# A graph layer on one core: SP takes one source tile in 64, ScalarE issues the edge attributes' loads

## The chip, the cores and the metric

The kernel runs on one core of a Trainium2 chip. A core has TensorE (PE, matrix products into PSUM), VectorE (DVE), ScalarE (ACT), GpSimd (POOL) and SyncE (SP), each with its own stream of instructions, and DMA engines that move data between DRAM and the core's SBUF. SP, ACT and POOL issue the DMAs. The metric is the time of one execution on the device in microseconds (us); before the change it is 4050.13, the median of 3 runs.

## The reference, cut to what matters

A message layer on a graph of N = 12500 nodes with C = 96 channels and E = 412500 directed edges, sorted by their target node (`col`), four attributes to an edge:

```
def mlp(h, W, b, gamma, beta):                       # relu, then a norm over all rows
    h = relu(h @ W + b)
    return gamma * (h - mean(h, 0)) * rsqrt(var(h, 0) + 1e-5) + beta
node = mlp(x, W_node, ...)                           # 12500 x 96
edge = mlp(edge_attr, W_edge, ...)                   # 412500 x 96, from 4 attributes
msg  = mlp(concat([x[src], x[col], edge], 1), W_msg, ...)
out  = layernorm(x + segment_sum(msg, col) + node)
```

The three parts of W_msg act apart from each other. So the kernel makes two tables first, p_tab = x W_1 and q_tab = x W_2, and a message is relu(p_tab[src] + q_tab[col] + edge part). Source nodes come in random order, so p_tab[src] has to be gathered row by row; target nodes are sorted, so a run of edges needs only a short window of q_tab.

## The kernel before, in words

Edges are taken in 3223 tiles of 128, one edge to a partition. Four tiles make a group (`GT`), four groups a block (`BG`): 806 groups, 202 blocks.

The gather is POOL's: one indirect DMA for each tile (L181) reads 128 rows of 96 numbers. The first 64 tiles are read from x itself, while p_tab isn't made yet; their product with W_1 is made later (`convert`). Gathered groups wait in a ring of 26 groups (`RING`, 13 buffers of two groups, named pg). So that POOL has work from the beginning, it gathers the first 104 groups (26 blocks, the early ones) while the tables and the statistics of the edges are made; SP writes them to DRAM (`spill`).

The main loop starts at about 619 us and takes 202 steps, one to a block. A late block's tiles come from the ring. An early block comes back from DRAM (`fetch`, buffer pb, one transfer on SP); an early block stands after about each seventh late one, so that 16 steps hold some 14 late ones and 2 early ones. `order` is this order.

For each group k of the loop:
- `linear(k + 3)`: PE makes z in PSUM (L507) from `left`, the edge part and the one-hot windows of the target nodes, and from `rhs`, the window of q_tab and the weights of the block. z has two buffers of a pair of groups; the first one's bank also holds `nodes_of`, a constant which DVE reads in L520.
- `message(k)`: DVE adds the gathered rows to z (L516), and in one group of each block builds the one-hot matrix `at` (L520).
- `first_part` (ACT L533), `clipped` (L539), `squared` (L543), `second_part` (DVE L568, ACT L569), `third_part` (DVE L574): a message is split into three bf16 parts, and its square is kept for the norm. These work on pairs of groups.
- `sums`: PE adds the messages by target node (L586).

At the start of step s, `load(s + 2)` issues what step s + 2 needs: in every second step the edge attributes ea of two blocks (four DMAs at L445, two at L447), and in every step the register with the block's first node (`base`) and the window of q_tab into `rhs` (L455), which has three slots. `edges` (PE L493) and `prepare` (ACT L501) turn ea into `left`.

SP helps POOL: in one group of `SG` = 20 it fetches the last tile itself, row by row, 128 DMAs of 384 bytes (`rows_of`, L623). They are spread out, 16 rows (`SR`) at every second group (`SS`), so eight such portions lie in 16 of the 20 groups; the node numbers are loaded into SP's registers 16 at a time (L619), from one row of the list that `row_numbers` loads into `wide`.

`manual_schedule` keeps the order of the instructions on SP, POOL, PE, DVE and ACT as the program writes them, each engine for itself. All DMAs of SP and ACT together share eight completion counters. They are dealt out when the program is built; each DMA waits for the one before it on its counter.

After the last group the norm of the messages is finished from `squares` and `total`: the last products, unread products that nobody reads (`unread`, L466 to L470), pd (L892), and the output of all nodes, py (L903) and what follows it.

Of the kernel before, what the change touches and what calls it, by code (L numbers as in the profile page):

```python
# [11 lines left out]
F32 = mybir.dt.float32  # L12
# [11 lines left out]
P = 128  # L24
# [3 lines left out]
GT, GE, BG = 4, 512, 4  # L28
# [30 lines left out]
NW = WS * (BG - 1) + WN + 1  # L59
OW = NW * GT + WS * (BG - 1)  # L60
CL, CE = 2, 2
BUSY = 2
J = 8
SR, SS = 16, 2
SG = 5 * BG


K, W, ROWS = 4, 128, 12672
# [11 lines left out]
def gnn(ctx, tc, t):  # L80
# [18 lines left out]
    for i in range(0, NB, CH):  # L99
        part = slice(i * P, (i + CH) * P)  # L100
        (nc.scalar if i // CH % 2 else nc.sync).dma_start(xp[:, part], t["xp"][:, part])
    nc.scalar.dma_start(src, t["src"])

    ident = const.tile([P, P], F32, name="ident")
    make_identity(nc, ident)
# [249 lines left out]
    def fast(ring):  # L355
# [45 lines left out]
        with tc.tile_pool(name="fix", bufs=1) as fix, tc.tile_pool(name="msg", bufs=2) as work, \  # L401
# [34 lines left out]
            def load(s):  # L436

                b = order[s]
                first = SPILL // BG
                c, o = ((b - first) // CL * CL + first, CL) if b >= first else (b // CE * CE, CE)  # L440
                if c not in eas:
                    o = min(o, NBL - c)
                    eas[c] = work.tile([P, o, GE], F32, name="ea" if b >= first else "eae", bufs=2 if b >= first else 1)
                    for i in range(BG):
                        nc.sync.dma_start(eas[c][Q * i:Q * i + EK, :, :], t["ea"][EK * i:EK * (i + 1), c:c + o, :])  # L445
                    for i in range(2):
                        nc.sync.dma_start(eas[c][EK + i:P:Q, :, :], rel_d[i][:, c * BG * GE:(c + o) * BG * GE]  # L447
                                          .rearrange("o (b g e) -> (o g) b e", g=BG, e=GE))
                ea = eas[c][:, b - c, :]
                _, val = nc.values_load_multi_w_load_instructions(  # L450
                    base[:, b:b + 1], engines=[ET.SP], min_val=0, max_val=N - 1,
                    skip_runtime_bounds_check_because="they are nodes' numbers")
                rows = q_tab[bass.ds(val[0], WN), :]
                rows = bass.AP(rows.tensor, rows.offset, [[C, WN], [WS * C, BG], [1, C]], None, rows.runtime_checks)
                nc.sync.dma_start(rhs[C:C + WN, s % RB, :, :], rows)  # L455
                block[s] = ea
# [7 lines left out]
                        got[b * BG + i] = back[:, i, :, :]  # L464

            def unread(n):  # L466
                busy = ps.tile([P, GE], F32, name="pa")
                for i in range(n):
                    nc.tensor.matmul(busy, ident, rel[:, i * P:(i + 1) * P, :].rearrange("p g t -> p (g t)"),
                                     start=True, stop=True)  # L470

            def convert(s):
# [69 lines left out]
            def squared(sq, m=2, n=GT):  # L542
                nc.scalar.activation(sq[:, :m, :n, :], sq[:, :m, :n, :], AF.Square)  # L543
                return sq, m, n
# [70 lines left out]

                nc.sync.dma_start(lin, t["rows"][g * GT + GT - 1:g * GT + GT, :])

            def rows_of(pg, lo, hi):
                _, val = nc.values_load_multi_w_load_instructions(  # L619
                    lin[:, lo:hi], engines=[ET.SP], min_val=0, max_val=N - 1,  # L620
                    skip_runtime_bounds_check_because="they are nodes' numbers")
                for p in range(lo, hi):
                    nc.sync.dma_start(pg[p:p + 1, GT - 1, :], p_tab[bass.ds(val[p - lo], 1), :])  # L623

            n, ahead = len(steps), SPILL + RING
            row_numbers(ahead)
            with tc.manual_schedule(engines={ET.SP, ET.Pool, ET.PE, ET.DVE, ET.Activation}):
                bad = nc.values_load(flag, min_val=0, max_val=1, skip_runtime_bounds_check_because="a comparison's result")
                load(0)
                fetch(0)  # L630
                load(1)
                fetch(1)
                for half in range(2):
                    edges(0, half)
                    prepare(0, half)
                edges(1, 0)
                for k in range(3):
                    linear(k)
                waiting, last = None, BG * (len(order) - 1)
                for k in range(last):  # L640
                    s, g = steps[k]
                    if g % BG == 0:
                        if s + 2 < len(order):
                            load(s + 2)
                            fetch(s + 2)
                    message(k)
                    j = k - LATER - BG - 1
                    if k % 2:
                        first_part(k - 1)
                        now = squared(clipped(k - 1))  # L650
                        if waiting:
                            moments(*waiting)
                        waiting = now
                        second_part(k - 1)
                    if j >= 0 and j % BG == 0:
                        fold(j // BG)
                    if j >= 2 and j % BG == 2:
                        add(j // BG, place(j // BG))
                    if k % 2:
                        third_part(k - 1)  # L660
                    if j >= 1 and j % BG == 1:
                        turn(j // BG)
                    if k >= LATER:
                        sums(k - LATER)
                    if g % BG != 3 and s + 1 < len(order):
                        if g % 2:
                            edges(s + 1, 1)
                        else:
                            prepare(s + 1, g % BG // 2)
                    if g % BG == 3:  # L670
                        if s + 1 < len(order) and order[s + 1] < RAW:
                            convert(s + 1)
                        if s + 2 < len(order):
                            edges(s + 2, 0)
                    if k + 3 < n:
                        linear(k + 3)
                    if g >= SPILL:
                        m = (ahead - SPILL - RING) % SG
                        if m == 0:
                            by_row = ahead if ahead + SG <= NG else None  # L680
                        got[ahead] = ahead_of(ahead, int(ahead == by_row))
                        if by_row is not None and m % SS == 0 and m // SS * SR < P:
                            lo = m // SS * SR
                            rows_of(got[by_row], lo, lo + SR)
# [9 lines left out]
                sq = clipped(last, 1, GT)  # L694
# [4 lines left out]
                unread(1)  # L699
# [3 lines left out]
                squared(sq, 1, GT)  # L703
                collect(sq[:, 0, :, :].rearrange("p t c -> p (t c)"), GT)
                third_part(last, 1, GT)
                sums(last)
                fold(s - 1)
                at_end = place(s - 1), place(s)
                sq = clipped(n - 1, 1, m)
                second_part(n - 1, 1, m)  # L710
                turn(s - 1)
                squared(sq, 1, m)
                collect(sq[:, 0, :, :].rearrange("p t c -> p (t c)"), m, r)
                add(s - 1, at_end[0])
                third_part(n - 1, 1, m)
                sums(n - 1)
                square_sum = ps.tile([P, 2, GE], F32, name="pr", bufs=1)[:C, 0, :1]
                fold(s)
                turn(s)
                nc.tensor.matmul(square_sum, squares, ones, start=True, stop=True)  # L720
# [240 lines left out]
```

## Time and profile before

| | |
|---|---|
| runs | 4050.13, 4064.94, 4049.47 us; median 4050.13 |
| profiled execution | 4065.14 us, its span 4063.7 us |
| granted TensorE clock, mean | 0.631 |
| busy: PE, DVE, ACT, POOL | 77%, 63%, 50%, 75% of the span |
| gathers on POOL | 3190, from 3.1 to 3997.7 us |
| row copies on SP | 4224, 616.3 to 3778.0 us |
| moved by DMA | 274.95 MB |

Lines of the profile name the engine, the source line, and the tensors written and read. Groups give busy time, the mean of one instruction, and the idle time before it with what ended that. A wait's line gives the total, how often, and the longest. Timeline and chain give the start, the length and what ran. Landings of DMAs (`DMA rhs<-q_tab`) are from the issue to the completion.

### The profile page before, as it was taken

Reading aid. Unit: us, or ns where it says so; the run is one execution under the profiler, and the core shown is the slowest. Engines: PE = TensorE matmul, PEld = TensorE weight load, DVE = VectorE, ACT = ScalarE, POOL = GpSimd, SP = SyncE. Lnnn points to the kernel's source line nnn. Section 1 sums busy time; section 2 is a strip of 40 time slices with the busy share of each in tenths; the row PEclk is TensorE's granted clock in tenths of the full one; section 3 lists DMA queues with packets and bytes.
Section 4 is the critical chain, followed back from the end, with each engine's and each line's share of the span. In section 5 each row is a group of like instructions: output and inputs, shape, how many; then the busy total and the mean of one; then the engine's idle time right before and its main releaser. Section 6 shows DMA issues by size and latency. Waiting matters only on the chain.

```text
span 4063.7 us, 56007 instructions
## 1 busy us (share of the span) xinstructions
PE 3140.1 (77%) x13544; PEld 2307.0 (57%) x13544; DVE 2572.9 (63%) x4036; ACT 2039.1 (50%) x2422; POOL 3038.6 (75%) x3219
## 2 busy tenths in 40 slices
PE   4699958888878877777777777786877777777777
PEld 3466636666656555555555555555555555555556
DVE  2599985667667755666566556665666556655665
ACT  1388844555555544544444444544554445444443
POOL 7777777777777777777777777777777777777774
PEclk7655556666666766666666666656666666666665
DMA  8555532222222222222222222222222222222233
GB/s 232 174 121 115 116 82 56 55 55 54 49 55 55 57 57 54 54 47 56 53 47 55 55 54 49 54 54 54 56 47 54 56 54 47 56 54 54 48 84 80
DMA packets 201673, 274.95 MB, mean 68 GB/s; under 512 B 129940, under 2 KB 130358, under 8 KB 200328
## 3 DMA queue, kind: packets, MB, share of 16 engines
q0 software_dynamic: 102080, 157.00, 19.3%
q1 hardware_dynamic: 85814, 105.62, 9.5%
q10 hardware_dynamic: 13440, 8.65, 0.8%
q8 instruction: 111, 1.82, 0.2%
q14 instruction: 228, 1.87, 0.2%
HBM read 227.58 MB, written 43.43 MB: 67 GB/s over the span
## 4 chain that ended last, share of the span: by engine, by line
POOL 38%; issue 19%; PE 16%; DMA 11%; DVE 8%; SPq 7%; ACT 1%; DVEq 0%; POOLq 0%; ACTq 0%
POOL pg L181 38%; DMA pg<-p_tab,src 8%; PE z L507 8%; SPq L623 5%; PE pa L586 4%; PE pr L493 3%; DVE sum_of L549 2%; DVE z L516 1%; DVE z L568 1%; SPq L619 1%; DVE h L574 1%; ACT h L569 1%; PE py L903 1%; DVE at L520 1%; DMA pg<-in_x,src_raw 1%
## 5 line engine op out<-in xcount | busy, mean ns | idle before, releaser
L181 POOL DMA_INDIRECT pg<-p_tab,src x3126 | 2953.9, 945 | 955.0 <-issue 885.7
L507 PEld LDWEIGHTS z<-rhs,left 128*128 128x128 f32 x6446 | 1276.4, 292 | 985.5 <-DVE h L574 825.6
L507 PE MATMUL z<-rhs,left 128*128 128x96 f32 x6446 | 1364.9, 383 | 547.4 <-DVE h L574 539.2
L586 PE MATMUL pa<-h,at 128*80 128x291 bf16 x3223 | 837.1, 406 | 161.2 <-DVE at L520 157.8
L533 ACT ACTIVATE h<-z 128x768 bf16<-128x768 f32 x404 | 330.2, 817 | 1193.9 <-DVE z L516 1189.4
L516 DVE TENSOR_TENSOR z<-z,pg 128x384 f32<-128x384 f32 x702 | 394.3, 562 | 648.7 <-DMA pg<-p_tab,src 624.4
L586 PEld LDWEIGHTS <-at 128*80 128x80 bf16 x3223 | 493.9, 167 | 271.1 <-DVE at L520 200.4
L501 ACT ACTIVATE left<-pr 127x1024 f32<-127x1024 f32 x403 | 411.1, 1020 | 419.0 <-PE pr L493 417.7
L549 DVE TENSOR_REDUCE sum_of<-sq 128x96 f32<-128x768 f32 x401 | 589.6, 1470 | 0.0
L493 PE MATMUL pr<-ea,we 7*127 7x512 f32 x1404 | 509.9, 809 | 49.0 <-DMA ea<-rel_d 43.8
L574 DVE TENSOR_TENSOR h<-z,h 128x768 bf16<-128x768 f32 x404 | 387.0, 958 | 243.8 <-ACT h L569 242.6
L568 DVE SCALAR_TENSOR_TENSOR z<-z,h 128x768 f32<-128x768 f32 x404 | 387.4, 959 | 64.0 <-ACT sq L539 64.0
L318 PE MATMUL pr<-ea,wide 10*128 10x512 f32 x1212 | 358.9, 1083 | 8.9 <-DMA ea<-in_ea 8.9
L324 DVE BATCH_NORM_STATS2 estats<-r 128x6 f32<-128x512 f32 x606 | 359.9, 675 | 7.9 <-ACT r L322 7.8
L569 ACT ACTIVATE h<-z 128x768 bf16<-128x768 f32 x404 | 329.2, 815 | 67.0 <-DVE z L568 66.5
L322 ACT ACTIVATE r<-pr 128x1024 f32<-128x1024 f32 x303 | 306.9, 1024 | 105.9 <-PE pr L318 62.8
L543 ACT ACTIVATE sq<-sq 128x768 f32<-128x768 f32 x404 | 339.7, 841 | 13.1
L520 DVE TENSOR_TENSOR at<-rel,z 128x496 bf16<-128x496 f32 x202 | 135.8, 672 | 307.8 <-PE z L507 307.7
L539 ACT ACTIVATE sq<-z 128x768 f32<-128x768 f32 x404 | 323.0, 799 | 0.3 <-DVE h L574 0.3
L318 PEld LDWEIGHTS pr<-ea,wide 10*128 10x128 f32 x1212 | 249.2, 309 | 117.3 <-issue 64.7
L493 PEld LDWEIGHTS pr<-ea,we 7*127 7x127 f32 x1404 | 134.9, 235 | 174.5 <-issue 141.2
L551 DVE TENSOR_TENSOR squares<-sum_of,squares 128x96 f32<-128x96 f32 x401 | 104.2, 260 | 13.8
(127 smaller groups left out, 1114.0 us busy)
## 6 DMA issues: line engine op xcount, KB each, us to landing
pg<-p_tab SPq DMA_DIRECT2D x4224, 0.4 KB
pg<-p_tab,src POOLq DMA_INDIRECT x3126
spill<-pg SPq DMA_DIRECT2D x52, 384.0 KB
pb<-spill SPq DMA_DIRECT2D x26, 768.0 KB
ea<-in_ea SPq DMA_DIRECT2D x75, 160.0 KB
rhs<-q_tab SPq DMA_DIRECT2D x202, 46.5 KB
ea<-in_ea SPq DMA_DIRECT2D x352, 20.0 KB
y_d<-y0s SPq DMA_DIRECT2D x12, 384.0 KB
```

The lines of the kernel that those rows point to most:

```text
L181: nc.gpsimd.indirect_dma_start(out=pg[:, i, :], out_offset=None, in_=tab[:, :], in_offset=bass.IndirectOffsetOnAxis(ap=idx[:, k:k + 1], ax ...
L318: nc.tensor.matmul(pr[:, k % 2, :], wide[Q * i:Q * i + 2 * EK, :], ea[Q * i:Q * i + 2 * EK, b % J, :], start=True, stop=True)
L324: nc.vector.bn_stats(stats[:, (k - o) % NS, (k - o) // NS, :], r[:, 1 - o, :])
L493: nc.tensor.matmul(prs[s, half][:C + WN, i, :], we[o:o + EK + 2, :], block[s][o:o + EK + 2, :], start=True, stop=True)
L501: nc.scalar.activation(x[:C + WN, 2 * half:2 * half + n, :], pr[:C + WN, :n, :], AF.Relu)
L507: nc.tensor.matmul(zb[k // 2 % 2][:, k % 2, i * C:(i + 1) * C], left[s % 2][:KR, g % BG, i * P:(i + 1) * P], rhs[:KR, s % RB, g % BG, :], ...
L516: nc.vector.tensor_add(z, z, got.pop(g)[:, :n, :])
L549: nc.vector.tensor_reduce(sum_of, sq[:, :m, :n, :].rearrange("p g t c -> p c g t"), axis=AX.XY, op=OP.add)
L568: nc.vector.scalar_tensor_tensor(z, z, 0.0, h[0], op0=OP.max, op1=OP.subtract)
L569: nc.scalar.activation(h[1], z, AF.Copy)
L574: nc.vector.tensor_tensor(h[2], z, h[1], op=OP.subtract)
L586: nc.tensor.matmul(pas[s][:NW, :3 * (C + 1)], at[s % HB][:r, i, o + NW * t:o + NW * (t + 1)], h[:r, t, :, :].rearrange("p a c -> p (a c)") ...
```

## The change

Four things are changed.

- `SG` goes from 20 groups to 16: SP fetches one tile in 64 instead of one in 80, 42 tiles instead of 33, or 5376 row copies instead of 4224, and POOL gathers 3181 tiles instead of 3190. The 32 numbers (`SV`) of two portions are loaded at once: 168 loads of 32 instead of 264 of 16.
- The edge attributes in the main loop, 606 DMAs, are issued by ACT instead of SP. The rhs loads and the reloads of early blocks stay on SP.
- x is loaded in 14 pieces, all issued by SP, instead of 7 in turns by SP and ACT; the list of all sources follows on SP instead of ACT.
- At the end, the order of the last group's work is another, the unread products are half as wide (256 columns) and more: 4, 1, 1 and 5 instead of 1 and 2; they are written to the bank of `pr`, and the sum of squares to a part of `pas`.

```
--- before.py
+++ after.py
@@ -59,10 +59,10 @@
 NW = WS * (BG - 1) + WN + 1
 OW = NW * GT + WS * (BG - 1)
 CL, CE = 2, 2
-BUSY = 2
+BUSY = 5
 J = 8
-SR, SS = 16, 2
-SG = 5 * BG
+SR, SS, SV = 16, 2, 32
+SG = 4 * BG
 
 
 K, W, ROWS = 4, 128, 12672
@@ -96,10 +96,10 @@
     ring = rpool.enter_context(tc.tile_pool(name="ring", bufs=RING // 2))
     xp = xpool.enter_context(tc.tile_pool(name="x", bufs=1)).tile([C, NN], F32, name="xp")
     nc.scalar.dma_start(w_msg, t["L0_gnn_W_msg"].rearrange("(s k) f -> k s f", k=C))
-    for i in range(0, NB, CH):
-        part = slice(i * P, (i + CH) * P)
-        (nc.scalar if i // CH % 2 else nc.sync).dma_start(xp[:, part], t["xp"][:, part])
-    nc.scalar.dma_start(src, t["src"])
+    for i in range(0, NB, CH // 2):
+        part = slice(i * P, min(i + CH // 2, NB) * P)
+        nc.sync.dma_start(xp[:, part], t["xp"][:, part])
+    nc.sync.dma_start(src, t["src"])
 
     ident = const.tile([P, P], F32, name="ident")
     make_identity(nc, ident)
@@ -442,9 +442,9 @@
                     o = min(o, NBL - c)
                     eas[c] = work.tile([P, o, GE], F32, name="ea" if b >= first else "eae", bufs=2 if b >= first else 1)
                     for i in range(BG):
-                        nc.sync.dma_start(eas[c][Q * i:Q * i + EK, :, :], t["ea"][EK * i:EK * (i + 1), c:c + o, :])
+                        nc.scalar.dma_start(eas[c][Q * i:Q * i + EK, :, :], t["ea"][EK * i:EK * (i + 1), c:c + o, :])
                     for i in range(2):
-                        nc.sync.dma_start(eas[c][EK + i:P:Q, :, :], rel_d[i][:, c * BG * GE:(c + o) * BG * GE]
+                        nc.scalar.dma_start(eas[c][EK + i:P:Q, :, :], rel_d[i][:, c * BG * GE:(c + o) * BG * GE]
                                           .rearrange("o (b g e) -> (o g) b e", g=BG, e=GE))
                 ea = eas[c][:, b - c, :]
                 _, val = nc.values_load_multi_w_load_instructions(
@@ -464,9 +464,9 @@
                         got[b * BG + i] = back[:, i, :, :]
 
             def unread(n):
-                busy = ps.tile([P, GE], F32, name="pa")
+                busy = ps.tile([P, 2, GE], F32, name="pr", bufs=1)[:, 0, :GE // 2]
                 for i in range(n):
-                    nc.tensor.matmul(busy, ident, rel[:, i * P:(i + 1) * P, :].rearrange("p g t -> p (g t)"),
+                    nc.tensor.matmul(busy, ident, rel[:, i * P:i * P + P // 2, :].rearrange("p g t -> p (g t)"),
                                      start=True, stop=True)
 
             def convert(s):
@@ -615,12 +615,15 @@
 
                 nc.sync.dma_start(lin, t["rows"][g * GT + GT - 1:g * GT + GT, :])
 
-            def rows_of(pg, lo, hi):
+            def addresses(lo, hi):
                 _, val = nc.values_load_multi_w_load_instructions(
                     lin[:, lo:hi], engines=[ET.SP], min_val=0, max_val=N - 1,
                     skip_runtime_bounds_check_because="they are nodes' numbers")
-                for p in range(lo, hi):
-                    nc.sync.dma_start(pg[p:p + 1, GT - 1, :], p_tab[bass.ds(val[p - lo], 1), :])
+                return val
+
+            def rows_of(pg, lo, val):
+                for p, v in enumerate(val):
+                    nc.sync.dma_start(pg[lo + p:lo + p + 1, GT - 1, :], p_tab[bass.ds(v, 1), :])
 
             n, ahead = len(steps), SPILL + RING
             row_numbers(ahead)
@@ -681,7 +684,9 @@
                         got[ahead] = ahead_of(ahead, int(ahead == by_row))
                         if by_row is not None and m % SS == 0 and m // SS * SR < P:
                             lo = m // SS * SR
-                            rows_of(got[by_row], lo, lo + SR)
+                            if lo % SV == 0:
+                                val = addresses(lo, lo + SV)
+                            rows_of(got[by_row], lo, val[lo % SV:lo % SV + SR])
                             if m // SS * SR == P - SR and by_row + 2 * SG <= NG:
                                 row_numbers(by_row + SG)
                         ahead += 1
@@ -691,32 +696,34 @@
                 collect(waiting[0].rearrange("p g t c -> p (g t c)"), 2 * GT)
                 message(last)
                 first_part(last, 1, GT)
-                sq = clipped(last, 1, GT)
+                sq = [clipped(last, 1, GT)]
                 turn(s - 2)
                 add(s - 2, place(s - 2))
                 sums(last - 2)
                 sums(last - 1)
-                unread(1)
+                unread(BUSY - 1)
                 second_part(last, 1, GT)
                 message(n - 1)
                 first_part(n - 1, 1, m)
-                squared(sq, 1, GT)
-                collect(sq[:, 0, :, :].rearrange("p t c -> p (t c)"), GT)
+                sq.append(clipped(n - 1, 1, m))
+                squared(sq[0], 1, GT)
                 third_part(last, 1, GT)
+                second_part(n - 1, 1, m)
+                collect(sq[0][:, 0, :, :].rearrange("p t c -> p (t c)"), GT)
                 sums(last)
                 fold(s - 1)
                 at_end = place(s - 1), place(s)
-                sq = clipped(n - 1, 1, m)
-                second_part(n - 1, 1, m)
+                unread(1)
                 turn(s - 1)
-                squared(sq, 1, m)
-                collect(sq[:, 0, :, :].rearrange("p t c -> p (t c)"), m, r)
+                squared(sq[1], 1, m)
+                collect(sq[1][:, 0, :, :].rearrange("p t c -> p (t c)"), m, r)
+                third_part(n - 1, 1, m)
                 add(s - 1, at_end[0])
-                third_part(n - 1, 1, m)
                 sums(n - 1)
-                square_sum = ps.tile([P, 2, GE], F32, name="pr", bufs=1)[:C, 0, :1]
+                unread(1)
                 fold(s)
                 turn(s)
+                square_sum = pas[s][:C, GE - P + NW:GE - P + NW + 1]
                 nc.tensor.matmul(square_sum, squares, ones, start=True, stop=True)
                 unread(BUSY)
                 mean_square = fix.tile([C, 1], F32, name="mean_square")
```

More of the change, by code (lines that the diff above doesn't have):

```diff
@@ L61 @@
 CL, CE = 2, 2
-BUSY = 2
+BUSY = 5
 J = 8
-SR, SS = 16, 2
-SG = 5 * BG
+SR, SS, SV = 16, 2, 32
+SG = 4 * BG
 K, W, ROWS = 4, 128, 12672
@@ L98, in gnn @@
     nc.scalar.dma_start(w_msg, t["L0_gnn_W_msg"].rearrange("(s k) f -> k s f", k=C))
[L99 to L102, printed above, removed]
+    for i in range(0, NB, CH // 2):
+        part = slice(i * P, min(i + CH // 2, NB) * P)
+        nc.sync.dma_start(xp[:, part], t["xp"][:, part])
+    nc.sync.dma_start(src, t["src"])
     ident = const.tile([P, P], F32, name="ident")
@@ L444, in load @@
                     for i in range(BG):
[L445 removed]
+                        nc.scalar.dma_start(eas[c][Q * i:Q * i + EK, :, :], t["ea"][EK * i:EK * (i + 1), c:c + o, :])
                     for i in range(2):
[L447 removed]
+                        nc.scalar.dma_start(eas[c][EK + i:P:Q, :, :], rel_d[i][:, c * BG * GE:(c + o) * BG * GE]
                                           .rearrange("o (b g e) -> (o g) b e", g=BG, e=GE))
@@ L466, in unread @@
             def unread(n):
-                busy = ps.tile([P, GE], F32, name="pa")
+                busy = ps.tile([P, 2, GE], F32, name="pr", bufs=1)[:, 0, :GE // 2]
                 for i in range(n):
-                    nc.tensor.matmul(busy, ident, rel[:, i * P:(i + 1) * P, :].rearrange("p g t -> p (g t)"),
+                    nc.tensor.matmul(busy, ident, rel[:, i * P:i * P + P // 2, :].rearrange("p g t -> p (g t)"),
                                      start=True, stop=True)
@@ L621, in rows_of @@
                     skip_runtime_bounds_check_because="they are nodes' numbers")
-                for p in range(lo, hi):
-                    nc.sync.dma_start(pg[p:p + 1, GT - 1, :], p_tab[bass.ds(val[p - lo], 1), :])
+                return val
+            def rows_of(pg, lo, val):
+                for p, v in enumerate(val):
+                    nc.sync.dma_start(pg[lo + p:lo + p + 1, GT - 1, :], p_tab[bass.ds(v, 1), :])
             n, ahead = len(steps), SPILL + RING
@@ L693, in fast @@
                 first_part(last, 1, GT)
-                sq = clipped(last, 1, GT)
+                sq = [clipped(last, 1, GT)]
                 turn(s - 2)
@@ L698, in fast @@
                 sums(last - 1)
-                unread(1)
+                unread(BUSY - 1)
                 second_part(last, 1, GT)
```

24 lines of the change are left out of this document (14 added, 10 removed).

## The prediction

> **What bounds the kernel now.** I read the busy shares first, then the costliest groups, then the waits of POOL, DVE, ACT and SP, and last the timeline and the chain of one stretch of the main loop (1190 to 1300 us).
>
> ```profile
> PE 3140.1 (77%) x13544; PEld 2307.0 (57%) x13544; DVE 2572.9 (63%) x4036; ACT 2039.1 (50%) x2422; POOL 3038.6 (75%) x3219
> ...
> L181 POOL DMA_INDIRECT pg<-p_tab,src x3126 | 2953.9, 945 | 955.0 <-issue 885.7
> ```
> ```profile
> ACT h L533 <- DVE z L516: 1189.4, 328, 9.9
> POOL pg L181 <- issue: 902.1, 2959, 0.3
> ...
> DVE z L516 <- DMA pg<-p_tab,src: 624.4, 218, 23.7
> ...
> DVE at L520 <- PE z L507: 307.7, 192, 6.0
> ...
> POOL pg L181 <- DMA pg<-p_tab,src: 40.4, 126, 1.1
> ```
> ```profile
> 1253.29 0.94 POOL L181 DMA_INDIRECT pg<-p_tab,src  x1 [0.30 <-issue]
> ...
> 1254.54 0.94 POOL L181 DMA_INDIRECT pg<-p_tab,src  x1 [0.30 <-issue]
> ```
>
> POOL is only 75% busy, but its idle time is 0.30 us of issue after each gather: a gather starts every 1.25 us, from 90.0 to 3997.7 us, and POOL waits for nothing else of size. Its consumers wait for it: DVE's addition L516 waits 624.4 us for gathered tiles. So POOL's count of gathers sets the time, as long as the consumer (PE, DVE, ACT, and SP behind them) keeps its pace. A step of 16 tiles is 16 x 1.248 = 20.0 us of POOL; 176 of the 202 steps (the late ones) need that, the 26 early ones, fed back from DRAM, need none.
>
> The consumer is not far ahead of that pace, and it starts behind:
>
> ```profile
> L181 POOL DMA_INDIRECT pg<-p_tab,src x420: 940/944/1937, 90.0 to 618.8; - x140
> L181 POOL DMA_INDIRECT pg<-in_x,src_raw x64: 940/944/3124, 3.1 to 88.8; - x64
> ```
> ```profile
> L516 DVE TENSOR_TENSOR z<-z,pg x702: 467/566/567, 619.2 to 4000.5; 128x384 f32<-128x384 f32 x176
> ```
> ```profile
> DVE z L516 <- DMA pg<-p_tab,src: 12.5, 4, 4.5
> ```
>
> At 619 us POOL has made 420 + 64 = 484 gathers, 68 more than the 416 of the early groups; so the first late tile is 68 x 1.25 = 85 us old when its message is added. Between 640 and 1190 us the waits of DVE show none for a gathered tile; the last row, of 1190 to 1480 us, is the first: the consumer needs some 800 us to catch up.
>
> **The change, part by part.**
>
> *Fewer gathers.* 42 tiles instead of 33 come by rows of SP; POOL has 9 gathers fewer: 9 x 1.248 = -11.2 us, if POOL stays the bound. The 1152 more row copies go to SP.
>
> *SP's own work.* Its rows, from the timeline, the chain and the groups of SP:
>
> ```profile
> 1263.33 0.27 SPq L455 DMA_DIRECT2D rhs<-q_tab  x1
> 1263.64 2.36 SPq L445 DMA_DIRECT2D ea<-in_ea  x4
> 1266.05 1.10 SPq L447 DMA_DIRECT2D ea<-rel_d  x2
> 1268.25 1.38 SPq L455 DMA_DIRECT2D rhs<-q_tab  x2
> 1276.61 14.63 SPq L623 DMA_DIRECT2D pg<-p_tab  x32
> ```
> ```profile
> 1226.14 0.80 SPq L450
> 1227.54 1.20 SPq L619
> ```
>
> Thirty-two rows with one register load of 1.20 us inside take 14.63 us, so a row takes (14.63 - 1.20) / 32 = 0.42 us. A step with rows cost SP 32 x 0.42 + 2 x 1.20 + 0.80 + 0.27 = 16.9 us, and each second step 3.5 us more for the six loads of edge attributes. After: each late step has rows (before, four of five), 13.4 + 0.80 + 0.27 and one load of 32 registers. That load is not in the trace: at least 1.20, at most 2.40 us; I take 1.20, as one instruction. That is 15.7 us (16.9 at the other end), under POOL's 20.0. By its own work alone SP gets no worse.
>
> *The loads on ACT's queue.* Six issues per load, some 2.4 to 3.5 us of SP, go to ACT, which is 50% busy. [...]
>
> [...] SP's and ACT's copies share eight completion counters, and each copy waits for the one before it on its counter. Before, in the loop, SP alone used them. Now 47 of the 99 loads in the loop look like this, in the order that the program was built in: the six copies sit on two counters, three deep, so ACT issues the third pair only when the second has landed, and SP's row 19 of 32 in step S-2 waits for a copy that ACT issues at the start of step S. Behind that row stand 13 more, then the base register and the weights rhs of step S+1. SP cannot run ahead of ACT any more. What waits for rhs is in the trace:
>
> ```profile
> 1263.33 4.47 DMA rhs<-q_tab
> 1267.94 2.01 PE z L507 x8
> ...
> 1330.48 2.16 DMA ea<-rel_d
> ```
> ```profile
> 1271.15 0.82 ACT L533 ACTIVATE h<-z 128x768 bf16<-128x768 f32 x1 [5.17 <-DVE z L516]
> ...
> 1273.70 0.82 ACT L569 ACTIVATE h<-z 128x768 bf16<-128x768 f32 x1 [0.16 <-DVE z L568]
> ...
> 1279.17 0.82 ACT L569 ACTIVATE h<-z 128x768 bf16<-128x768 f32 x1 [0.17 <-DVE z L568]
> ...
> 1286.83 0.82 ACT L569 ACTIVATE h<-z 128x768 bf16<-128x768 f32 x1 [0.17 <-DVE z L568]
> ...
> 1292.32 0.82 ACT L569 ACTIVATE h<-z 128x768 bf16<-128x768 f32 x1 [0.19 <-DVE z L568]
> ```
>
> A late rhs (issued 1263.33, landed 1267.80) released PE's z at 1267.94, then DVE's L520, which reads the same bank as that z (it waits for z in 192 of 202 steps), and with it the last pair of groups of the step before: its L569 ended at 1274.52, 6.7 us after the landing. There ACT starts the next step. Two pairs with nothing late take 1292.32 - 1279.17 = 13.2 us; I use 14 for a step.
>
> So from one load to the next, two late steps on, the chain is:
> - three landings on ACT: each 2.16 us where the chain shows one. The chain shows only those late enough to count, so I take 1.7: 5.1 us (ends 0 and 6.5);
> - SP's 14 rows, 5.9; base and rhs, 1.1; one register load, 1.2; 32 rows, 13.4; base and rhs, 1.1: 22.7 us;
> - rhs landing, 4.47 where it counted; I take 4.0;
> - to the end of the step, 6.7 us.
>
> Sum 38.5 us (40.4 at the upper end, 33.4 with no hold) against 2 x 20.0 = 39.9 of POOL. Alone that would just do. But early steps come on top: two in 16, with no gather of their own to pay for them. Over 16 steps (steps 109 to 124 of the new order, two early) I add, by the waits of each load in the built program: a load one step before the next load, 5.1 + 5.9 + 1.1 + 4.0 + 6.7 = 22.8; two of 38.5; one whose second step follows an early one and so has its rhs in time, 22.8 + 14 = 36.8; two where SP meets the copies only in the rows of step S-1 and rhs is in time, 2 x 14 and about 2 for ACT's hold, 30 each; one that holds SP from row 5 on (23 rows behind it, so 9 x 0.42 and some more), 43.6; one that lets SP off at row 27, 34.4; a step between two loads, 15.3. Sum 22.8 + 77 + 36.8 + 60 + 43.6 + 34.4 + 15.3 = 290 us, 18.1 a step. POOL needs 14 x 20.0 = 280 for them. The rows end about ten steps before the last. Consumer: 619 + 192 x 18.1 + 10 x 14 = 4234 us for the last message instead of 4000: +234 us. The 9 gathers are then hidden.
>
> *x and src on SP.* What the start needs last of x is p_tab:
>
> ```profile
> 65.50 10.70 DMA p_tab<-trow
> ...
> 90.05 0.94 POOL pg L181
> ```
>
> Its last store lands at 76.2, the first gather from it starts at 90.05: 13.9 us of cover. I cost it at 0. If the cover went, POOL would start p_tab's gathers later by what is over 13.9 us; a gain is at most what POOL waits in its start. I keep -5 to +5 for the range.
>
> *The end.*
>
> ```profile
> 3997.69 2.64 DMA pg<-p_tab,src
> ...
> 4006.26 3.62 PE pa L469 x4
> ...
> 4010.56 41.29 PE py L903 x192
> ```
> ```profile
> 4010.50:4053.00 42.50, 42.13 (x196) 41.89 (x196) 22.41 (x35) 12.52 (x23) 14.47 (x10) 0.50 0.33 85
> ```
>
> Four unread passes of 512 columns took 3.62 us ahead of the last matrix products. Now five products of half the width, ten passes, stand there: 10 x 0.45 = 4.5, +0.9 us, and two more earlier in gaps; the reordered pieces are each under 1 us. I take +1, between -15 and +3. The -15 is the clock: py ran at a granted clock of 0.50, and the runs lie in two places, 4049.47 and 4050.13 against 4064.94, which fits a py at a higher clock. The profiled execution, 4065.14, is of the upper kind. [...]
>
> **Sum.** In the profiled execution 4065.1 + 234 + 1 = 4300; carried to the median, which lies 15.0 below it, 4285.
>
> **The rivals.**
> 1. *Covered* (the other side): the coupling costs less than POOL's slack. For it: without any hold the pair of steps takes 33.4 us against 39.9, DVE waits 624.4 us for gathers, ACT is half idle. It decides where 16 steps take at most 264 us (16.5 a step: 619 + 192 x 16.5 + 140 = 3927, with room for the raw blocks of the start), that is 26 less than my sum, over nine loads and steps some 3 us each: landings of 0.7 us instead of 1.7 on ACT. Then time falls by the gathers: 4050.1 - 11.2 + 1 = 4040. With a start or a tail a little better it reaches below 4030.
> 2. *Pace kept, lag not closed*: 16.9 to 17.2 us a step. The consumer keeps about POOL's pace, but what it starts behind stays open: 619 + 192 x 16.9 + 140 = 4004 to 4061, +4 to +61: 4055 to 4110, say 4085.
> 3. *ACT becomes the bound*: the holds on ACT add to its pairs in every load, as if most loads held SP from row 5 on (43.6 us): 19.5 us a step, 619 + 192 x 19.5 + 140 = 4503, +503: 4550. Against it: ACT's own work is 50%.
>
> **How the numbers follow.** Forecast (18.1 a step, own range 4110 to 4440 for 17.2 to 18.9): 0.50. Rival 1: 0.32, of which 0.09 below 4030 and 0.23 within 0.5% (20 us, about what a measurement tells from no change). Rival 2: 0.12, a quarter of it within 0.5%. Rival 3: 0.06. Faster 0.09; same 0.23 + 0.03 = 0.26; slower 0.50 + 0.09 + 0.06 = 0.65. Range: from 4032, which leaves out the better part of rival 1, to 4440, which leaves out rival 3 and the full landings.
>
> **What would show it.** Right: POOL's gathers get gaps beyond 0.30 us, waiting for a freed ring buffer (DVE z L516); SP waits long for DMA ea; ACT gets waits for DMA at L445 or L447; PE and DVE's L520 wait for rhs; DVE's wait for pg falls far below 624 us; x and end move by a few us. Wrong: POOL's pace stays at 1.25 us to the end and the last gather starts near 3986; then the hold was short or SP was not late, and the step that failed is the chain of 38.5 us. If py's clock changes, the last 45 us say so.

## The result: 7.8% slower

The changed kernel takes 4376.32 us (median of 6, 4373.88 to 4383.62). The kernel before took 4065.08 us beside it, and the ratio is 1.078, with an interval of 1.0759 to 1.0802. Against the 4050.13 us of the prediction that is 326 us more; 4285 was forecast, with 4032 to 4440 as the range. The runs of the kernel before lie in two places, some 4047 to 4055 us ("lower" below) and some 4064 to 4073 ("upper"), and 4065.08 is of the upper one. The profiled execution has a span of 4374.4 us.

These are the waits of the changed kernel, all engines and then SP (line, what it waited for, us in total, how often, the longest). L626 is the row copy, L623 before.

```profile
ACT h L533 <- DVE z L516: 1159.1, 211, 13.7
DVE at L520 <- PE z L507: 976.7, 201, 12.0
POOL pg L181 <- issue: 891.8, 2924, 0.6
...
PE z L507 <- DMA rhs<-q_tab: 758.9, 122, 13.4
...
POOL pg L181 <- DVE z L516: 261.0, 60, 15.3
...
ACT left L501 <- DMA ea<-rel_d: 183.2, 42, 5.5
```
```profile
SPq L626 <- DMA ea<-in_ea: 335.0, 52, 15.8
SPq L626 <- DMA ea<-rel_d: 289.5, 38, 21.5
...
SPq L626 <- DMA eae<-rel_d: 72.1, 11, 7.7
```

PE's wait for rhs in the kernel before:

```profile
PE z L507 <- DMA rhs<-q_tab: 6.7, 4, 3.0
```

Three things are new. SP's rows wait about 700 us for the edge attributes that ACT issues. PE waits 759 us for rhs, where it was 6.7, and behind it L520, from 308 to 977 us. And POOL, which waited for nothing of size, waits 261 us for L516: its ring is full and a buffer comes free only when a message has been added. The reverse wait is gone: L516 waited 624 us for gathered tiles before. Its two rows now, the first with durations and the first and last start, the second from the list of groups (busy, mean ns, idle before and what ended most of it):

```profile
L516 DVE TENSOR_TENSOR z<-z,pg x702: 467/558/567, 612.4 to 4325.5; 128x384 f32<-128x384 f32 x176
```
```profile
L516 DVE TENSOR_TENSOR z<-z,pg 128x384 f32<-128x384 f32 x702 | 392.4, 559 | 26.8 <-PE z L507 20.2
```

The first gives the first and the last message: 612.4 and 4325.5, where it was 619.2 and 4000.5. The loop is 332 us longer; the start is 7 us shorter and what follows the last message 14 us (48.9 instead of 63.2 to the end of the span). The consumer is the bound now, not POOL.

The chain of waits between 2036 and 2062 us shows how (start, length, what ran), from one load of ACT to the next:

```profile
2037.30 1.84 DMA ea<-in_ea
2039.15 2.02 DMA ea<-in_ea
2041.19 2.00 DMA ea<-rel_d
2043.20 0.22 SPq L626
...
2048.43 0.22 SPq L626
...
2048.69 0.53 SPq L450
...
2049.47 4.24 DMA rhs<-q_tab
2053.72 0.14 issue
2053.85 2.01 PE z L507 x8
2055.88 0.07 DVE at L520
...
2059.62 2.01 DMA eae<-in_ea
```

Three landings one behind the other, SP's remaining 14 rows, the base register, rhs, z, L520, the rest of the pair, and ACT is at its next load: 22.3 us. The trace also names the semaphore on which each copy counts. SP's and ACT's copies use the same eight: between 620 and 4200 us all 5570 of SP and all 576 of ACT wait on the semaphore on which they count, and on each side 279 come on it right behind a copy of the other engine. In the kernel before, SP's 5100 copies from 620 us on are alone on theirs. The six copies of this load sit on two of them, three deep, and the row at 2043.20 is the next copy on the semaphore of the three landings.

### The profile page after: what moved, and what is told of

Same layout as the page of the kernel before. It is cut to its first block, busy times and chain, and to the rows that moved or that the text cites. A ratio compares the mean times of both kernels' runs of the same rounds, so it can differ in the third digit from the quotient of the medians.

```text
span 4374.4 us, 59399 instructions
## 1 busy us (share of the span) xinstructions
PE 3115.9 (71%) x13560; PEld 2282.3 (52%) x13560; DVE 2564.4 (59%) x4036; ACT 2034.2 (47%) x2422; POOL 3031.8 (69%) x3210
## 3 DMA queue, kind: packets, MB, share of 16 engines
q14 instruction: 255, 2.09, 0.2%
## 4 chain that ended last, share of the span: by engine, by line
DMA 22%; SPq 20%; DVE 20%; PE 14%; issue 14%; POOL 8%; ACT 2%; ACTq 0%; DVEq 0%; POOLq 0%
SPq L626 16%; POOL pg L181 8%; DVE estats L324 8%; PE z L507 7%; DMA rhs<-q_tab 7%; DMA ea<-in_ea 6%; DVE sum_of L549 3%; DMA pg<-p_tab,src 3%; DVE z L568 2%; PE pa L586 2%; DVE z L516 2%; PE pr L493 2%; SPq L619 2%; DMA ea<-rel_d 2%; SPq L450 1%
## 5 line engine op out<-in xcount | busy, mean ns | idle before, releaser
L501 ACT ACTIVATE left<-pr 127x1024 f32<-127x1024 f32 x403 | 411.7, 1021 | 782.5 <-PE pr L493 358.1
L520 DVE TENSOR_TENSOR at<-rel,z 128x496 bf16<-128x496 f32 x202 | 135.8, 672 | 976.7 <-PE z L507 976.7
L516 DVE TENSOR_TENSOR z<-z,pg 128x384 f32<-128x384 f32 x702 | 392.4, 559 | 26.8 <-PE z L507 20.2
```

Source lines behind the costliest of these rows:

```text
L501: nc.scalar.activation(x[:C + WN, 2 * half:2 * half + n, :], pr[:C + WN, :n, :], AF.Relu)
L516: nc.vector.tensor_add(z, z, got.pop(g)[:, :n, :])
```

## The experiments

A word that is used below: a row's distance is how many steps ahead of it the load of ACT stands for which it waits. It is read from the built program, since the counters are dealt out there; counted by the semaphores in the traces, the numbers below come out the same.

**ACT's loads back on SP, all else changed.**

```
- nc.scalar.dma_start(eas[c]...      (L445, L447)
+ nc.sync.dma_start(eas[c]...
```

> The changed kernel, but SP issues the edge attributes' loads again; asked once more, since on the chip of the runs before all instruction streams paused and the kernel before took over 6200 us. On a chip on which the kernel before takes some 4050 to 4065 us. Theory (SP's rows wait for ACT's copies): the slowdown is gone, 4030 to 4060 us, PE's wait for rhs under 50 us. Rivals (the larger number of rows, or the loads of 32 registers): 4250 us or more.

Measured: 4036.36 us (10 runs, 4034.71 to 4038.29), before 4049.53; ratio 0.9954 (0.9938 to 0.9970). The slowdown is gone with this one edit. In the profile PE's wait for rhs is 33 us, and POOL has its pace again:

```profile
PE z L507 <- DMA rhs<-q_tab: 32.8, 13, 6.5
```
```profile
POOL pg L181 <- issue: 901.7, 2955, 1.0
```
```profile
L181 POOL DMA_INDIRECT pg<-p_tab,src x3117: 938/944/3324, 83.1 to 3984.6; - x195
```

The last gather starts at 3984.6 instead of 3997.7. Both rivals, the rows or the larger register loads as the cause by themselves, fall: SP carries both here, and the loads of ea as well. The time hides what they cost, though. PE now waits for ea, and DVE's wait for gathered tiles, the cover, falls from 624 to 343 us:

```profile
PE pr L493 <- DMA ea<-rel_d: 207.6, 32, 12.5
```

In the kernel before that wait was 43.8 us.

**The rows alone.** The kernel before, with 42 tiles by rows and 32 numbers to a load.

```
- SG = 5 * BG                 + SG = 4 * BG;  SV = 32
- rows_of(pg, lo, lo + SR)    + val = addresses(lo, lo + SV) at every second portion
```

> The kernel before with one part of the change alone: one tile in 64 by rows and registers loaded 32 at a time; the loads of ea stay on SP, x and the end as before. Theory: POOL stays the bound, nine gathers fewer: 11 us less than the kernel before at the same clock of the last products, 4038 or 4053 us. The difference to the run with all of the change but ACT's loads (4036 us) is then x and the end. Rival (those 13 us came from x and the end alone): equal to the kernel before.

Measured: 4043.55 us (10 runs; 7 of them 4041.70 to 4044.23, 3 of them 4058.77 to 4060.66), before 4050.26; ratio 0.9982 (0.9961 to 1.0002). At the lower place that is some 7 us less, where 11 were expected; the last gather starts at 3989.0, 8.7 earlier. The other 6 us of the run above are by difference those of x and the end. DVE's wait for gathered tiles is 423 us here: the rows use up some 200 us of cover without costing time.

**ACT's loads alone.** The kernel before, with only the edge attributes' loads on ACT.

```
- nc.sync.dma_start(eas[c]...
+ nc.scalar.dma_start(eas[c]...
```

> The kernel before with one part of the change alone: ACT issues the edge attributes' loads; 33 tiles by rows, registers 16 at a time, x and the end as before. Theory (SP's rows wait for copies that ACT issues): slow by itself. In its build fewer loads hold a row two steps back than in the changed kernel, and one step in five has no rows: 4110 to 4300 us, with SP's rows waiting for ea and PE waiting for rhs. Rival (it takes the larger number of rows too): within 20 us of the kernel before.

Measured: 4049.74 us (10 runs), before 4050.26; ratio 0.9998 (0.9978 to 1.0019). The expectation of 4110 to 4300 was wrong, and the rival right: alone, this part costs nothing. But the mechanism is there, as the waits of SP, PE and DVE show:

```profile
SPq L623 <- DMA ea<-in_ea: 547.8, 81, 18.8
```
```profile
PE z L507 <- DMA rhs<-q_tab: 335.5, 68, 11.5
...
DVE z L516 <- DMA pg<-p_tab,src: 151.0, 67, 4.7
```

PE waits 336 us for rhs, where it was 6.7. What pays is DVE's waiting for gathered tiles, 624 us before and 151 here. The consumer still keeps POOL's pace, so the time stays.

**All of the change but the number of rows.**

```
- SG = 4 * BG
+ SG = 5 * BG
```

> The changed kernel with one part undone: one tile in 80 by rows again (33 tiles), the register loads of 32, ACT's loads, x and the end as changed. In its build a row of step s waits for ACT's load of step s or s+1 in 239 of 348 waits, of s+2 in 109. Theory (more rows put SP further behind in the build, and only two steps behind is too far): POOL keeps its pace, 4035 to 4065 us, PE's wait for rhs at 200 to 450 us but hidden. Rival (ACT's loads with the registers of 32, x or the end are enough for the slowdown): 4200 us or more.

Measured: 4045.91 us (8 runs, 4043.35 to 4048.16), before 4068.16 (6 of 11 runs at the upper place; the middle one of the other five is 4052.34); ratio 0.9956 (0.9938 to 0.9975). Its waits are those of the run above (PE for rhs 339 us, rows for ea 512 us), and hidden as there. So neither part does it alone. Nor do the two prices add up to it: ACT's loads alone used up 473 us of DVE's 624 and the rows alone 201, together 50 more than there was, but the loop became 332 us longer. My reading is that ACT's loads put a price on SP being behind, and that the rows decide how far behind: of the waits of rows for ACT's loads, 109 of 348 have distance two here, 196 of 285 in the changed kernel. Of ACT's 101 loads 70 hold a row two steps back in the changed kernel, 47 here, 44 with ACT's loads alone. No run gives SP and ACT counters of their own, which would be the direct test.

**Half as many loads.** The changed kernel, with the edge attributes of four late blocks in each load of ACT.

```
- CL, CE = 2, 2
+ CL, CE = 4, 2
```

> The changed kernel, but ACT loads the edge attributes of four late blocks at once instead of two: half as many loads, each in six copies of twice the size; the early blocks' loads are as they were. The counters stay shared. Theory (each load of ACT holds SP's rows once): with half the holds the slowdown of some 320 us falls by more than half, as POOL's pace needs only a part of them gone: 4040 to 4190 us; SP's wait for ea about half of 710 us. Rival (SP is too slow for its rows whatever ACT does, or ACT's bytes count): 4300 us or more.

Measured: 4250.17 us (4 runs, 4241.20 to 4265.97), before 4050.26; ratio 1.049 (1.0448 to 1.0534). Of some 326 us, 126 are gone, less than half; 4040 to 4190 was expected. The rival, 4300 or more, does not hold either. SP's rows wait 542 us for ACT's loads in the two longest entries (469.1 for ea, 72.4 for eae), where about half of 710 was expected. So the number of holds alone does not set the loss: of 57 loads, 47 hold a row two steps back, no more than in the run before this one, which lost nothing; but 28 of these begin at the seventh of a step's 32 rows, where in the changed kernel 47 of 70 begin at the nineteenth, and so more rows stand behind the hold. One more wait is larger than in the changed kernel:

```profile
ACT left L501 <- DMA pg<-p_tab: 428.6, 37, 13.0
```

ACT's copies also wait for rows of SP on the shared counters: 429 us here, 96 us in the changed kernel. I had not expected this direction to grow. No run tells what each of the two is worth.

**rhs four steps ahead.** The changed kernel, with rhs in five slots.

```
- load(s + 2)      # ea and rhs
+ load(s + 2)      # ea
+ window(s + 4)    # base register and rhs;  RB = 5
```

> The changed kernel, but the window of q_tab for rhs is loaded four steps ahead instead of two, into five slots instead of three. The loads of ea stay on ACT, SP's rows still wait for them, the counters are still shared. Theory (the harm is that rhs stands behind the held rows, two steps ahead being too little): 4030 to 4070 us; PE's wait for rhs from 759 to under 60 us, DVE's L520 on z back to 300 to 400, SP's waits of rows for ea stay at 300 us or more, ACT still waits at its loads. Rival (the hold of ACT at its own loads, some 4 to 5 us each, makes the steps long): still above 4250 us.

Measured: 4439.01 us (4 runs), before 4050.26; ratio 1.096 (1.0915 to 1.0997). Slower than the changed kernel. PE's wait for rhs fell to 65 us as expected, and something else took its place:

```profile
DVE z L519 <- DMA pb<-spill: 550.2, 22, 34.1
```
```profile
PE z L510 <- DMA rhs<-q_tab: 65.0, 11, 9.9
```
```profile
SPq L629 <- DMA ea<-in_ea: 582.1, 101, 19.9
```

DVE waits 550 us for pb, the reload of an early block, which stands on SP behind the rows too and is still asked for two steps ahead. So my theory in its first form, that asking earlier cures it, did not hold. The built program shows what I had missed: with rhs ahead, 266 of the 403 waits have distance three. Given more slack, SP's rows stand further behind ACT's loads, and the waits fix that for the chip. My explanation is that the build deals out the counters by its own timing, in which SP falls behind until something stops it, and that what stopped it was rhs two steps ahead; no run shows this step.

**pb ahead too.** The test between the two forms of the theory.

```
- fetch(s + 2)
+ fetch(s + 4)
```

> The kernel with rhs four steps ahead, and now the early blocks' reload (pb) four steps ahead too; ACT still issues ea. Theory, as first put (what stands on SP behind held rows comes late because it is asked for too late): with both ahead, 4030 to 4130 us. Theory, as changed by the run before (how far SP's rows stay behind ACT is dealt out when the program is built: in the changed kernel a row of step s waits for ACT's load of step s+2 in 196 of 285 waits, with rhs ahead of step s+3 in 266 of 403, here of s+3 or s+4 in 287 of 317; so the lateness grows with what is given): still slow, 4250 to 4500 us, with rows of late tiles, rhs or pb late in their turn.

Measured: 4356.65 us (4 runs, 4336.17 to 4362.65), before 4068.16; ratio 1.071 (1.0660 to 1.0751). Still slow, as the second form said and the first did not. Of the 317 waits, 287 now have distance three or four. The wait for pb is gone from the list of the longest, and rhs is late again although it is asked for four steps ahead:

```profile
PE z L510 <- DMA rhs<-q_tab: 566.5, 89, 12.8
```

**Five runs on a chip that pauses.** The first five runs landed on a chip on which the kernel before took 6214 to 6228 us. I didn't find the cause. ACT and DVE stop there again and again for about 10 us where the trace names no releaser of this core (in the first of the five, ACT's L501 waits 1336 us in 106 such pauses, DVE's L516 872 us in 101); the kernel before has no such wait in its profile on the other chip. Where the expectations say that all instruction streams paused, the traces show it of ACT, DVE and SP; POOL's longest gap without a wait is 8.4 to 8.5 us in the first four runs, against 0.3 in the kernel before on the other chip, and for PE they leave it open.

> The changed kernel with one part undone: SP issues the edge attributes' loads again; the rows, the register loads of 32, x, the end and the unread products stay changed. Theory (SP's rows wait for copies that ACT issues two steps later in the order, and so rhs comes late): the slowdown is gone, POOL's pace of 1.25 us holds to the end, 3181 gathers, 4030 to 4060 us; PE's wait for rhs falls from 759 us to under 50. Rival (the rows themselves, 5376 instead of 4224, keep SP from issuing rhs in time): still slow, 4250 us or more, with SP busy and not waiting. Rival (the loads of 32 registers, 2.1 us instead of 1.2): the same as the second.

Measured: 6532.88 us, before 6228.12 (ratio 1.050, 1.0472 to 1.0533).

> The kernel before with one part of the change alone: ACT issues the edge attributes' loads; 33 tiles by rows, registers 16 at a time, x and the end as before. Theory: slow by itself; fewer of its loads hold SP two steps back than in the changed kernel, and one step in five has no rows: 4110 to 4300 us, with SP's rows waiting for ea and PE waiting for rhs. Rival (it takes the larger number of rows too): within 20 us of the kernel before.

Measured: 6272.14 us (1.009, 1.0056 to 1.0115).

> The changed kernel, but the window of q_tab for rhs is loaded four steps ahead instead of two, into five slots instead of three. The loads of ea stay on ACT, SP's rows still wait for them, the counters are still shared. Theory (the harm is that rhs stands behind the held rows, two steps ahead being too little): 4030 to 4070 us; PE's wait for rhs from 759 to under 60 us, DVE's L520 on z back to 300 to 400, SP's waits of rows for ea stay at 300 us or more, ACT still waits at its loads. Rival (the hold of ACT at its own loads, some 4 to 5 us each, or the DMAs' rivalry, makes the steps long): still above 4250 us.

Measured: 6764.64 us (1.086, 1.0821 to 1.0894).

> The kernel before with one part of the change alone: one tile in 64 by rows and registers loaded 32 at a time; the loads of ea stay on SP, x and the end as before. Theory: POOL stays the bound, nine gathers fewer, 11 us faster than the kernel before, 4038 to 4055 by the state of the last products' clock. Rival (SP, with 13.4 us of rows, 2.1 us of registers, 1.1 and, in each second step, 3.5 us of loads in every late step, is full and rhs is late): 20 to 150 us slower.

Measured: 6529.71 us (1.050, 1.0466 to 1.0525).

> The same kernel as in the run before on a chip that stalls all instruction streams (there the kernel before took 6228 us): the changed kernel, but SP issues the edge attributes' loads again. Theory (SP's rows wait for ACT's copies): the slowdown is gone, 4030 to 4060 us, PE's wait for rhs under 50 us. Rivals (the larger number of rows, or the loads of 32 registers): 4250 us or more.

Measured: 6530.76 us, before 6214.45 (1.050, 1.0448 to 1.0549). SP's timeline of this run, two portions of 32 rows each:

```profile
2032.31 28.03 SPq L626 DMA_DIRECT2D pg<-p_tab  x32
...
2066.92 13.29 SPq L626 DMA_DIRECT2D pg<-p_tab  x32
```
```profile
POOL pg L181 <- DVE z L516: 2049.5, 185, 40.8
```

One portion takes 13.29 us, as elsewhere, the other 28.03, with a pause in it. POOL waits 2050 us for its ring, so the consumer is the bound, and there more rows on SP cost 5% by themselves (the fourth run), which they don't on the other chips. These runs answer nothing on the question, which is about a kernel bound by POOL.

## Why the prediction was right, and where it was off

*POOL as the bound before, and 9 gathers for -11.2 us.* Right in kind, where POOL stays the bound, and somewhat less in size. With the rows alone the last gather starts 8.7 us earlier. With ACT's loads back on SP it is 13.1 us, but 6.9 of these stand already at the first gather from p_tab, which comes from x.

*SP gets no worse by its own work.* Right for the time: 4036 us with all of it on SP. In its waits it does get worse, as PE's 208 us for ea show, and POOL's slack covers that. The price of the register load was at the other end of its bounds, though:

```profile
L619 SPq TENSOR_LOAD <-wide x168: 2022/2085/2265, 600.2 to 4215.3; - x168
```

2.09 us for 32 numbers, where I took 1.20 (1.20 to 2.40), and 1.22 us was the median for 16. So a load of 32 saves 0.36 us on two of 16, and no more.

*Rows of SP wait for ACT's copies; rhs comes late; L520 and the pair wait; ACT's next load.* Right, place by place, as the chain above shows. The terms beside the forecast: three landings 5.9 us (5.1 taken, 6.5 the upper end); 14 rows 5.5 (5.9); base and rhs to its issue 0.8 (1.1); rhs landing 4.24 (4.0); from there to ACT's next load 5.9 (6.7). The sum is 22.3 for the 22.8 of a load one step before the next.

*The pace.* 18.1 us a step for 192 steps and 14 for ten were forecast, 17.9 on the mean; measured (4325.5 - 612.4) / 202 = 18.4. Two terms are behind that. The first is the longer pair of steps, forecast at 38.5. Two loads of ACT that are two steps apart, and what SP did between them:

```profile
1929.11 2.86 ACTq L445 DMA_DIRECT2D ea<-in_ea  x4
...
1971.16 2.71 ACTq L445 DMA_DIRECT2D ea<-in_ea  x4
```
```profile
1942.39 0.27 SPq L455 DMA_DIRECT2D rhs<-q_tab  x1
1942.71 0.72 SPq L462 DMA_DIRECT2D pb<-spill  x1
1946.04 13.98 SPq L626 DMA_DIRECT2D pg<-p_tab  x32
1960.85 0.28 SPq L455 DMA_DIRECT2D rhs<-q_tab  x1
```

They are 42.1 us apart. Between the two rhs SP takes 18.5 us, where the forecast had 1.2 + 13.4 + 1.1 = 15.7: the register load is 0.9 us of the difference, the 32 rows 0.6, and the rest is mostly the reload of an early block (L462), which I had left out of the chain. The 16 steps of the forecast (109 to 124) show it term by term, from one load of ACT to the next (the first starts at 2651.25 us), as I match them by the rows that wait:

| load issued at step | forecast us | measured us |
|---|---|---|
| 109 | 38.5 | 41.3 |
| 111 | 36.8 | 36.5 |
| 113 | 30 | 29.4 |
| 115 (three steps) | 38.5 + 15.3 | 57.0 |
| 118 | 43.6 | 42.1 |
| 120 | 30 | 30.6 |
| 122 | 34.4 | 36.7 |
| 124 | 22.8 | 22.6 |
| sum | 290 | 296 |

The two of 38.5 are 6 us too small, which is nearly all of the difference. The term of 43.6 counts 23 rows, where a hold from row 5 on leaves 28 to issue; with these it would be some 44.

The second term was not in the sum at all. Four early blocks were gathered from x, and their product with W_1 is made in the loop (`convert`), on the chain of waits, four rounds to a block:

```profile
771.81 0.87 PE pr L478 x4
772.70 0.60 ACT xt L480
773.35 1.15 PE pr L482 x8
774.58 0.57 DVE pb L484
...
787.68 0.57 DVE pb L484
```

That is 16.4 us for one block. The pairs of steps that hold these blocks (from ACT's loads at 624.72, 747.46, 894.25 and 1066.55) took 49.2, 56.4, 54.2 and 53.9 us, where such pairs later take some 41. The prediction had room for these blocks in its first rival and put them at nothing in its own sum. The first 32 steps took 19.5 us each (612.4 to 1236.9) and so 45 us more than forecast, the next 160 took 18.5 each (to 4190.3) and 57 more; the start and the last ten steps give 11 back. That is the 91 us by which the last message came later than the 4234 forecast.

*The end.* +1 us was taken, with -15 as the other bound: against the profiled execution it was -14.3. The windows of the last products show the granted clock (the third number from the right, before the DMA share and GB/s), of the changed kernel and of the one with ACT's loads back on SP:

```profile
4333.00:4360.00 27.00, 22.26 (x198) 21.96 (x196) 22.01 (x36) 13.44 (x23) 15.08 (x11) 0.94 0.52 134
```
```profile
3990.00:3995.00 5.00, 4.52 (x23) 3.16 (x21) 2.80 (x16) 0.79 (x3) 1.66 (x5) 1.00 0.00 0
3995.00:4022.00 27.00, 22.17 (x197) 21.96 (x196) 22.45 (x36) 13.43 (x23) 15.52 (x11) 0.98 0.52 134
```

Clock 0.94 and 0.98 instead of 0.50, and 22 us of py instead of 42. The median that I compared with had this already, since by the profiles the two places are those of this clock. Two kernels with the old end, the rows alone (profiled at 4044.23 us) and ACT's loads alone (at 4068.46):

```profile
4001.00:4028.00 27.00, 22.12 (x196) 21.96 (x196) 22.54 (x36) 13.44 (x23) 15.69 (x11) 0.99 0.53 136
```
```profile
4013.00:4055.00 42.00, 41.64 (x196) 41.41 (x195) 21.60 (x33) 12.45 (x22) 13.22 (x10) 0.50 0.33 85
```

But the upper place is gone with the new end: none of the 18 runs of the two kernels with the new end at POOL's pace lies in it, where 21 of 49 runs of the kernel before do, and 7 of 20 of the two kernels with its end. The forecast has a cost of 0.9 us for more unread products and no gain. They may be what changed the clock, but the order of the last work changed with them, and no run separates the two. Being busy alone did not bring PE the higher clock: in the window from 3990 to 3995 us above it is busy 4.52 of 5.00 us at 1.00, and in the kernel before 42.13 of 42.50 us at 0.50.

*x on SP.* 0 was taken, within 5 us. The first message comes at 612.4, 611.6 and 617.8 in three runs with it, 618.6 to 619.6 in three without: a gain of 1 to 8 us. The first gather from p_tab starts at 85.9, 85.7 and 83.1 us instead of 90.0 to 91.6. What of this reaches the end is open: with 33 tiles by rows the last gather starts at 3997.6, as before.

*The rivals.* "Covered" is what happens with 33 tiles by rows: both such runs stay at POOL's pace. I had put its threshold on the size of the hold; by the runs it lies in how many steps, and how many rows, SP is behind. As the range held most of this rival too, the time alone would not tell the two apart; the waits and the chain do. "Pace kept" did not happen. "ACT becomes the bound" did not either: it was put at 19.5 us a step, and 192 steps took 18.6 each.

*What the move of the loads cost.* Moving 606 copies from SP to ACT cost 340 us (4376 against 4036). By the waits above, the copies of the two engines waited for each other on the counters that both use: SP's rows about 700 us for ACT's loads, ACT's copies 96 us for SP's rows.

## What to carry to other kernels

When DMAs move to another engine's queue, look in the built program at which counters both queues share, and which copy of the one waits for which of the other; how far apart they stand is fixed there, and asking earlier for the data did not help here (4439 and 4357 us against 4376), where the distance grew with it. A queue that carried both bulk work and something the next step needs was at risk here exactly then: the rows alone cost no time, the loads on ACT alone cost none, and both together cost 8%. Before a test of a part alone is taken for its price in the whole, see how much cover the whole still has: DVE's 624 us of waiting for POOL paid for ACT's loads once.

## What the runs showed that I had not expected

- A register load of 32 numbers takes 2.09 us and one of 16 takes 1.22.
- With the new end, which has eleven unread products of 256 columns instead of three of 512, the clock of py was 0.94 and 0.98 in two profiles, and the runs lost their second place 15 us up.
- Holding goes both ways on shared counters: ACT waited 429 us for rows of SP where its loads were half as many.
- One chip ran the same kernel in 6214 to 6228 us instead of 4050, with pauses of ACT and DVE that nothing on the core explains, and there a change of the rows that gains 7 us elsewhere cost 5%.

The best version found is the changed kernel with the edge attributes' loads left on SP: 4036.36 us, 0.5% under the kernel before. Some of that is the clock of py, as the median beside it mixes the two places; against the lower one, 4048.5, it is 0.3%.
